# Layer 0's denominators and normalised tokens turned by VectorE instead of TensorE, its projection placed at the next block's end, and layer 1's query rows copied by ScalarE

## The chip, the cores and the metric

The kernel runs on one core of a Trainium2 chip. The metric is the device time of the whole program in microseconds: 2126.64 us is the median of three runs of the kernel before (2126.23 to 2128.68). The span of its profile is 2126.2 us. A core has TensorE (PE, matmuls; its weight loads are listed apart as PEld), VectorE (DVE), ScalarE (ACT), GpSimd (POOL), and a sync engine (SP) that issues most transfers. The engines work through their own instructions in order and wait for one another through semaphores.

## The reference, cut to what matters

The input x is 4 images of 128 channels and 64 x 64 = 4096 tokens, all float32. Two layers of attention follow each other, and then a recurrent layer.

```python
# layer 0: attention over all tokens, 64 channels, residual in channel layout
att = jax.nn.softmax(jnp.einsum('bmi,bmj->bij', k, q), axis=2)
out = x + jnp.einsum('cm,bmn->bcn', wo, jnp.einsum('bij,bmj->bmi', att, v))
...
# layer 1: causal attention over normalised tokens, 128 channels
t = t + _L1_attn_ref(_ln_t(t), L1_attn_Wq, L1_attn_Wk, L1_attn_Wv)
# then a normalisation, a batch norm of W x and a scan over the tokens
t = t + _L1_ffn_ref(_ln_t(t), L1_ffn_W, L1_ffn_V, L1_ffn_gamma, L1_ffn_beta)
```

`_ln_t` subtracts the mean and divides by the standard deviation over the 128 channels of one token. What the change touches is the end of layer 0's attention: each token's weighted sum of values is projected by `wo`, divided by its softmax denominator and added to the token, and the result is normalised for layer 1.

## The kernel before, in words

`fast_path` (from L350) is what runs here. For each of the four batches it goes through layer 0 and then layer 1 in blocks of 512 queries, eight blocks per layer (g = 0 to 7). A block consists of items; an item is a pair of key tiles of 128 keys each, so p, the exponentials of one item, is 128 x 1024 for full tiles. Layer 0 has 16 items in each block. Layer 1 is causal and has 2, 4, ... 16 items in blocks 0 to 7; its last two items cross the diagonal and are narrower.

Every item passes through four steps:

- `scores` (L741 in layer 0, L750 in layer 1): TensorE multiplies keys by queries into a PSUM pair, of which there are two. Layer 0 has 64 channels only, so it uses 64 x 64 tiles of the array, four at a time.
- the exp by ScalarE (L755, L757) into p, which has four buffers (`prob`, bufs=4). In layer 1 GpSimd masks the diagonal (L761).
- `sums` (L779 the first item of a block, L781 the others): VectorE adds p up into `dsum`, from which the softmax denominators come.
- `values` (L801, L809): TensorE multiplies values by p and accumulates in `acc`, which has one buffer.

At the end of a layer-0 block ScalarE copies `acc` to `half` (L820), VectorE adds its two halves into `agg` (L821) and the two halves of `dsum` into `den` (L825). `den` is 128 x 512: it still has to be summed over the 128 partitions for each of 512 queries, and the result has to stand with a query on each partition.

The order of the work is that of the loop at the end of `fast_path`'s attention part. One turn of it is a slot. In slot s it emits the scores of item s, the values of item s - 2, then, where that item was the last of its block, `rows()` (the queries of the block after the next), `tokens()` (the load of tokens), and one task from the list `fill`; then it pushes the block's finishing chain (`finish0` or `finish1`). After that come the sums of item s and at most one due step of a finishing chain, or else one task of `side` (keys and values of the next batch). A chain is a generator; the number that it yields with a step says how many slots later the step is due. The framework then settles the place of each instruction on its engine; it may bring an instruction ahead of others on the same engine.

Before the change, `finish0` has one step, due two slots after the block's end: `project`, then `norm`. In layer 0 `project` has TensorE transpose `den` in four 128 x 128 pieces (L572), VectorE sums them from PSUM (L573) and takes reciprocals (L574); TensorE multiplies `agg` by `wo` (L577) and VectorE scales and adds to the tokens in `xs` (L582). `normed` takes mean and variance (L591, L592), has GpSimd raise the variance to the power -0.5 (L455), refines this by a Newton step on VectorE (L456 to L459), and writes normalised tokens `xh` (L598). At the next block's end the task from `fill` has TensorE transpose `xh` (L606), and ScalarE copies it to `xhT` (L607). In layer 1 `xhT` serves as keys and, multiplied by `g1` in `rows1` (L548, copied by VectorE, L550), as queries.

In layer 1 `project` already goes another way: VectorE transposes `den` in squares of 32 x 32 (L561), sums each (L563, `part`, 128 x 16), TensorE adds up the four partition groups with the constant matrix `fold` (L564), and VectorE picks the own group (L566, L569). Layer 1's normalised tokens go through squares as well: `second` in `finish1` transposes squares (L674, `sqT`), and DMAs write them to DRAM as `by_c` and read them back (L679, L683) so that the squares come to their places.

All of `r_ps`, `den_ps`, `o_ps`, `xhT_ps`, `wx_ps` and the tiles of keys and values come from one PSUM pool with two buffers (`misc`).

Of the kernel before, what the change touches and what calls it, by code (L numbers as in the profile page):

```python
# [9 lines left out]
F32 = mybir.dt.float32  # L10
AF = mybir.ActivationFunctionType
ALU = mybir.AluOpType
AX = mybir.AxisListType
PSUM = bass.MemoryType.PSUM

P = 128
BLK = 512
# [332 lines left out]
def fast_path(  # L350
# [21 lines left out]
    nc = tc.nc  # L372
# [5 lines left out]
    TPB = BLK // P  # L378
# [5 lines left out]
    S = nc.vector.STREAM_SQUARE_SIZE  # L384
    Q = P // S
# [4 lines left out]
    dram2 = ctx.enter_context(tc.tile_pool(name="dram2", bufs=2, space=bass.MemoryType.DRAM))  # L390
# [24 lines left out]
    ident = const.tile([P, P], F32, name="ident")  # L415
# [10 lines left out]
    fold = const.tile([P, P], F32, name="fold")  # L426
# [6 lines left out]
    quarter = const.tile([P, TPB, Q], F32, name="quarter")  # L433
# [27 lines left out]
    with tc.tile_pool(name="batch", bufs=1) as batch, tc.tile_pool(name="rows", bufs=2) as rowp, tc.tile_pool(  # L461
        name="prob", bufs=4
    ) as prob, tc.tile_pool(name="work", bufs=2) as wk, tc.tile_pool(name="stat", bufs=4) as stat, tc.tile_pool(
        name="ps_s", bufs=2, space=PSUM
# [81 lines left out]
        def rows1(b, g):  # L546
            ps = misc("r_ps")
            nc.tensor.matmul(ps, lhsT=g1, rhs=bs[b].xhT[:, ts(g, BLK)], start=True, stop=True)  # L548
            r = rowp.tile([P, BLK], F32, tag="r", name="rows1")
            nc.vector.tensor_copy(r, ps)  # L550
            bs[b].next.append(r)

        def project(layer, b, g, agg, den):

            dp = misc("den_ps")
            rec = recs[:, layer, b, ts(g, TPB)]
            if layer:


                sq = wk.tile([P, TPB * Q, S], F32, tag="sq", name="sq")  # L560
                nc.vector.transpose(out=sq.rearrange("p a b -> p (a b)"), in_=den)  # L561
                part = stat.tile([P, TPB * Q], F32, tag="part", name="part")
                nc.vector.tensor_reduce(part, sq, AX.X, ALU.add)  # L563
                nc.tensor.matmul(dp[:, : TPB * Q], lhsT=fold, rhs=part, start=True, stop=True)  # L564
                own = stat.tile([P, TPB, Q], F32, tag="own", name="own")
                nc.vector.tensor_tensor(  # L566
                    own, dp[:, : TPB * Q].rearrange("p (j q) -> p j q", q=Q), quarter, ALU.mult
                )
                nc.vector.tensor_reduce(rec, own, AX.X, ALU.add)  # L569
            else:  # L570
                for j in range(TPB):
                    nc.tensor.transpose(dp[:, ts(j, P)], den[:, ts(j, P)], ident)  # L572
                nc.vector.tensor_reduce(rec, dp.rearrange("p (j k) -> p j k", k=P), AX.X, ALU.add)  # L573
            nc.vector.reciprocal(rec, rec)  # L574
            op = misc("o_ps")
            for j in range(TPB):
                nc.tensor.matmul(  # L577
                    op[:, ts(j, P)], lhsT=agg[:, ts(j, P)], rhs=wv1 if layer else wo2, start=True, stop=True
                )
            for j in range(TPB):  # L580
                t = xs[:, b, ds(g * BLK + j * P, P)]
                nc.vector.scalar_tensor_tensor(  # L582
                    t, in0=op[:, ts(j, P)], scalar=rec[:, j : j + 1], in1=t, op0=ALU.mult, op1=ALU.add
                )
# [17 lines left out]
        def transposed(src, dst, name, engine):  # L602

            ps = misc(name)
            for j in range(TPB):
                nc.tensor.transpose(ps[:, ts(j, P)], src[:, j], ident)  # L606
            engine(dst, ps)  # L607

        def in_range():

            r = recs.rearrange("p l b t -> p (l b t)")
            r2 = wk.tile([P, BLK], F32, tag="den", name="r2")[:, : 2 * B * NT]
            nc.vector.tensor_scalar(r2, r, LOW, None, ALU.is_ge)
            nc.vector.tensor_scalar(r, r, HIGH, None, ALU.is_le)
            nc.vector.tensor_tensor(r, r, r2, ALU.mult)
            nc.vector.tensor_reduce(good, r, AX.X, ALU.add)
# [8 lines left out]
        def finish0(b, g):  # L625

            agg, den = bs[b].agg, bs[b].den

            def norm():
                if g == 0:  # L630
                    bs[b].xh = batch.tile([P, NT, P], F32, tag="xh", name="xh")
                    bs[b].xhT = batch.tile([P, N], F32, tag="xhT", name="xhT")
                normed(b, g, bs[b].xh[:, ts(g, TPB)])

            yield 2, lambda: (project(0, b, g, agg, den), norm())
            fill.append(
                lambda: transposed(bs[b].xh[:, ts(g, TPB)], bs[b].xhT[:, ts(g, BLK)], "xhT_ps", nc.scalar.copy)
            )

        def finish1(b, g):  # L640
            agg, den = bs[b].agg, bs[b].den
            mem = {}
            final = b == B - 1 and g == NB - 1

            def warm(n, rhs):

                ps = ps_s.tile([P, 2 * BLK], F32, tag="s", name="warm_ps")
                for _ in range(n):
                    nc.tensor.matmul(ps[:, : BLK // 2].rearrange("p (a c) -> p a c", c=P) if len(rhs.shape) == 3 else ps[:, : BLK // 2], lhsT=ident, rhs=rhs, start=True, stop=True)

            def first():
                if final:

                    nc.scalar.activation(spare, agg[:, 0:1], AF.Sigmoid)
                project(1, b, g, agg, den)
                if final:
                    warm(9, agg[:, : BLK // 2])
                nc.sync.dma_start(
                    out=x2[b, ts(g, BLK)].rearrange("(j p) c -> p j c", p=P),
                    in_=xs[:, b, ts(g, BLK)].rearrange("p (j c) -> p j c", c=P),  # L660
                )
                mem["xh"] = wk.tile([P, TPB, P], F32, tag="xh2", name="xh2")
                normed(b, g, mem["xh"])

            def second():
                mem["xhT"] = wk.tile([P, BLK], F32, tag="xhT2", name="xhT2")
                if final:
                    transposed(mem["xh"], mem["xhT"], "xh2T_ps", nc.vector.tensor_copy)
                    warm(1, mem["xh"][:, 2:])
                    return  # L670


                sq = wk.tile([P, Q, TPB, S], F32, tag="sqT", name="sqT")
                nc.vector.transpose(  # L674
                    out=sq.rearrange("p c j t -> p j c t"), in_=mem["xh"].rearrange("p j (c r) -> p j c r", r=S)
                )
                by_c = dram2.tile([Q, S, Q, P], F32, tag="by_c", name="by_c")
                for q in range(Q):
                    nc.sync.dma_start(  # L679
                        out=by_c[:, :, q].rearrange("c r k -> r c k"),  # L680
                        in_=sq[ts(q, S)].rearrange("r c j t -> r c (j t)"),
                    )
                nc.sync.dma_start(out=mem["xhT"], in_=by_c.rearrange("c r q k -> (c r) (q k)"))  # L683

            def third():
                wp = misc("wx_ps")
                nc.tensor.matmul(wp, lhsT=wf, rhs=mem["xhT"], start=True, stop=True)
                if b == B - 1 and g == NB - 1:
                    in_range()
                nc.vector.bn_stats(ends[:, 3:] if final else stats[:, b * NB + g], wp)  # L690
                if b == B - 1 and g == NB - 2:
                    ahead()

                to = xs[:, b, ts(g, BLK)]
                if final:
                    nc.scalar.copy(to.rearrange("p (s c) -> p s c", c=CPB), wp.rearrange("p (c s) -> p s c", s=STEPS))
                    warm(6, to[:, : BLK // 2])
                else:
                    nc.scalar.copy(  # L699
                        to.rearrange("p (s j q u) -> p s j q u", q=Q, j=TPB, s=STEPS),  # L700
                        wp.rearrange("p (q j u s) -> p s j q u", q=Q, j=TPB, s=STEPS),
                    )

            yield 1, first
            yield 3, second
            yield 1 if final else 4, third
# [123 lines left out]
        def push(slot, chain):  # L830
            step = next(chain, None)
            if step:
                waiting.append((slot + step[0], step[1], chain))
# [39 lines left out]
        for s in range(len(items) + SKEW + 16):  # L873
# [8 lines left out]
            if 0 <= s - SKEW < len(items):  # L882
                it = items[s - SKEW]
                values(it)
                if it.last:
                    rows()
                    tokens()
                    if fill:
                        fill.pop(0)()
                    push(s, (finish1 if it.layer else finish0)(it.b, it.g))  # L890
            if s < len(items):
                sums(items[s])
# [174 lines left out]
```

## Time and profile before

| what | from | value |
|---|---|---|
| span of the profiled execution | page | 2126.2 us |
| ScalarE, exps of layer 0, 512 of 128 x 1024 | L755 | 1117 ns each |
| VectorE, sums, 676 of 128 x 1024 | L781 | 1224 ns each |
| VectorE, denominators from PSUM, layer 0 | L573 | 684 ns x 32 |
| VectorE, squares of den, layer 1 | L561 | 711 ns x 32 |
| VectorE, sums of the squares, layer 1 | L563 | 677 ns x 32 |
| VectorE, own group, and its sum, layer 1 | L566, L569 | 169 and 168 ns x 32 |
| VectorE, squares of tokens, layer 1 | L674 | 711 ns x 31 |
| copy of r: VectorE | L550 | 680 ns x 32 |
| copy of the transposed tokens: ScalarE, same shape | L607 | 596 ns x 32 |
| TensorE, transposes of den and of tokens | L572, L606 | 128 each |

In a row of a timeline the first number is the start in us from the start of the span, the second the duration, then come engine, line, operation, what is written from what, the shape, and how many instructions are merged into the row. What stands in brackets is the idle time of the engine before it and who ended it. A float32 matmul counts as two records. Records of consecutive matmuls overlap in time, so that the distance of two starts says what the first cost, not its duration. In a row of stretches each engine has the us in which it was busy and the number of instructions.

### The profile page before, as it was taken

The numbers are of one execution on the slowest core, as the hardware profiler recorded it, in microseconds if no ns is written. First come the engines' busy times: TensorE is split into PE (matmuls) and PEld (weight loads), VectorE is DVE, ScalarE is ACT, GpSimd is POOL, SyncE is SP. The second block draws the span as 40 slices with busy tenths as digits, with TensorE's granted clock in tenths as the row PEclk, the third lists the DMA queues.
The fourth block names the chain that finished last, engine by engine and source line by source line (L and its number), as shares of the span: only waits on it lengthen the run. The fifth ranks groups of instructions, "written<-read, shape, count | busy, mean of one in ns | idle before, by whom it ended". The sixth has DMA issues, their size and how long they took to land. (4 is left out here: it accounts for less than half of the span.)

```text
span 2126.2 us, 30582 instructions
## 1 busy us (share of the span) xinstructions
PE 2102.6 (99%) x12072; PEld 931.3 (44%) x12072; DVE 1467.1 (69%) x2810; ACT 1009.4 (47%) x1099; POOL 110.2 (5%) x220
## 2 busy tenths in 40 slices
PE   9999999999999999999999999999999999999998
PEld 3333354444333344444333335444433334544456
DVE  4888865555888876544688887555478887755478
ACT  5666633233666643323466663332356664332355
POOL 1000000000000000000000001000000000100000
PEclk9999999999999999999999999999999999999999
DMA  3100022000100002100010002200000000110043
GB/s 110 41 1 2 1 60 60 15 15 16 55 2 1 2 21 69 35 25 15 16 41 1 2 1 60 60 15 15 15 16 1 1 2 1 45 30 15 15 164 160
DMA packets 66167, 64.98 MB, mean 31 GB/s; under 512 B 5617, under 2 KB 54257, under 8 KB 64993
## 3 DMA queue, kind: packets, MB, share of 16 engines
q1 hardware_dynamic: 65008, 62.41, 9.4%
q8 instruction: 96, 1.57, 0.3%
q14 instruction: 55, 0.44, 0.1%
q0 software_dynamic: 288, 0.39, 0.1%
q10 hardware_dynamic: 720, 0.16, 0.0%
HBM read 33.85 MB, written 24.90 MB: 28 GB/s over the span
## 5 line engine op out<-in xcount | busy, mean ns | idle before, releaser
L781 DVE TENSOR_TENSOR dsum<-dsum,p 128x1024 f32<-128x1024 f32 x676 | 827.3, 1224 | 454.1 <-ACT p L757 319.0
L755 ACT ACTIVATE p<-s_ps,nshift 128x1024 f32<-128x1024 f32 x512 | 572.0, 1117 | 349.4 <-PE s_ps L741 330.4
L757 ACT ACTIVATE p<-s_ps 128x1024 f32<-128x1024 f32 (+2 forms) x288 | 274.7, 954 | 563.7 <-PE s_ps L750 538.5
L801 PE MATMUL acc<-p,v 64*64 64x512 f32 x4096 | 533.9, 591 | 1.7 <-ACT half L820 1.7
L741 PE MATMUL s_ps<-kr 64*64 64x512 f32 x2048 | 530.4, 595 | 0.0
L741 PE MATMUL s_ps<-swap,kr 64*64 64x512 f32 x2048 | 530.4, 595 | 0.0
L750 PE MATMUL s_ps<-rows,xhT 128*128 128x512 f32 (+3 forms) x1152 | 503.1, 559 | 1.4 <-DVE rows L550 1.4
L809 PE MATMUL acc<-p,xh 128*128 128x512 f32 (+3 forms) x1152 | 501.5, 557 | 0.0
L809 PEld LDWEIGHTS acc<-p,xh 128*128 128x128 f32 x1152 | 215.6, 190 | 241.3 <-issue 231.8
L750 PEld LDWEIGHTS s_ps<-rows,xhT 128*128 128x128 f32 x1152 | 212.9, 190 | 242.3 <-issue 196.2
L801 PEld LDWEIGHTS acc<-p,v 64*64 64x64 f32 x4096 | 155.3, 133 | 286.1 <-issue 267.1
L741 PEld LDWEIGHTS s_ps<-swap,kr 64*64 64x64 f32 x2048 | 136.8, 133 | 132.4 <-issue 124.0
L741 PEld LDWEIGHTS s_ps<-kr 64*64 64x64 f32 x2048 | 136.9, 133 | 128.3 <-issue 123.7
L455 POOL TENSOR_TENSOR ln_rstd<-ln_var,mhalf 128x4 f32<-128x4 f32 x64 | 65.8, 1028 | 1086.5 <-DVE ln_var L594 1075.6
L789 DVE TENSOR_TENSOR dsum<-dsum,p 128x256 f32<-128x256 f32 (+1 forms) x120 | 55.9, 500 | 74.3 <-POOL p L761 74.3
L582 DVE SCALAR_TENSOR_TENSOR xs<-o_ps,recs,xs 128x128 f32<-128x128 f32 x256 | 72.5, 345 | 9.1 <-PE o_ps L577 3.1
L598 DVE TENSOR_SCALAR xh<-xs,ln_mv,ln_rstd 128x128 f32<-128x128 f32 x256 | 71.4, 344 | 2.2
L761 POOL TENSOR_SCALAR_AFFINE_SELECT p<-p 128x128 f32<-128x128 f32 x128 | 34.6, 294 | 665.5 <-ACT p L757 651.9
L591 DVE BATCH_NORM_STATS2 ln_st<-xs 128x6 f32<-128x128 f32 x256 | 63.7, 273 | 0.0
L779 DVE COPY dsum<-p 128x1024 f32<-128x1024 f32 x60 | 41.4, 690 | 29.8 <-ACT p L757 26.6
L699 ACT COPY xs<-wx_ps 128x512 f32<-128x512 f32 x31 | 18.2, 587 | 83.3 <-DVE stats L690 76.4
L964 DVE SCALAR_TENSOR_TENSOR z<-xs,scale,y_ps 128x256 f32<-128x256 f32 x108 | 48.3, 481 | 3.4 <-PE y_ps L962 1.9
(138 smaller groups left out, 1068.7 us busy)
## 6 DMA issues: line engine op xcount, KB each, us to landing
xs<-in_xT SPq DMA_DIRECT2D x32, 256.0 KB, 3.0
x<-xs SPq DMA_DIRECT2D x32, 256.0 KB, 2.2
xr<-x SPq DMA_DIRECT2D x8, 1024.0 KB, 12.1
out_x<-xr SPq DMA_DIRECT2D x16, 512.0 KB, 3.4
by_c<-sqT SPq DMA_DIRECT2D x124, 64.0 KB, 1.7
xhT<-by_c SPq DMA_DIRECT2D x31, 256.0 KB, 2.7
xs<-in_x SPq DMA_DIRECT2D x12, 512.0 KB, 5.5
swap<-kr SPq DMA_DIRECT2D x32, 128.0 KB, 2.2
```

What stands on the lines that cost most here:

```text
L455: nc.gpsimd.tensor_tensor(y, var, mhalf[:, : y.shape[-1]], ALU.pow)
L582: nc.vector.scalar_tensor_tensor(t, in0=op[:, ts(j, P)], scalar=rec[:, j : j + 1], in1=t, op0=ALU.mult, op1=ALU.add)
L591: nc.vector.bn_stats(st[:, j], xs[:, b, ds(g * BLK + j * P, P)])
L598: nc.vector.tensor_scalar(dst[:, j], xs[:, b, ds(g * BLK + j * P, P)], mv[:, j, 0:1], y[:, j : j + 1], ALU.subtract, ALU.mult)
L741: nc.tensor.matmul(ps[c * M : c * M + M, off : off + n], lhsT=bs[it.b].kr[part, h, ds(t % (NT // 2) * P + c * M, M)], rhs=rows[h], start=True,
L750: nc.tensor.matmul(ps[:, off : off + n], lhsT=lhsT, rhs=rhs, start=True, stop=True)
L755: nc.scalar.activation(it.p[:, :off], ps[:, :off], AF.Exp, bias=nshift)
L757: nc.scalar.activation(it.p[:, :off], ps[:, :off], AF.Exp, scale=float(P) ** -0.5)
L781: nc.vector.tensor_tensor(flat, flat, it.p, ALU.add)
L789: nc.vector.tensor_tensor(den[:, h, q0:], den[:, h, q0:], it.p[:, o : o + n], ALU.add)
L801: nc.tensor.matmul(bt.acc[h * M : h * M + M, r], lhsT=bt.v[part, t], rhs=it.p[part, o : o + n], start=it.first, stop=it.last,)
L809: nc.tensor.matmul(bt.acc[:, 0, q0:], lhsT=bt.xh[:, t], rhs=it.p[:, o : o + n], start=it.first and h == 0, stop=it.last and h == 1,)
```

## The change

The first four parts concern what follows a layer-0 block, the last one layer 1:

- `folded` holds the squares of `den` and their sums, which stood in layer 1's `project`; layer 0 now uses it too. `project` takes its result `part` in both layers, and the four transposes of `den` on TensorE and the reduce from PSUM go.
- `finish0`'s first step, one slot after the block's end, is `folded` alone; the projection is put into `fill` and so comes at the next block's end, between the last values of that block and the next scores.
- The norm follows one slot after the projection, and the transposition of the tokens two slots after that.
- Tokens are transposed in squares by VectorE (`squares`, which layer 1's `second` now calls too), and four DMAs write them to `by_r` in DRAM in pieces of 32 values (128 B), four more read `xhT` from there. The four transposes on TensorE and the copy by ScalarE go.
- `rows1` has ScalarE copy r, not VectorE.

Its purpose is to take transposes off TensorE, which the profile shows busy 99% of the span.

```diff
             r = rowp.tile([P, BLK], F32, tag="r", name="rows1")
-            nc.vector.tensor_copy(r, ps)
+            nc.scalar.copy(r, ps)
...
-        def project(layer, b, g, agg, den):
+        def folded(den):
+            sq = wk.tile([P, TPB * Q, S], F32, tag="sq", name="sq")
+            nc.vector.transpose(out=sq.rearrange("p a b -> p (a b)"), in_=den)
+            part = stat.tile([P, TPB * Q], F32, tag="part", name="part")
+            nc.vector.tensor_reduce(part, sq, AX.X, ALU.add)
+            return part
+        def project(layer, b, g, agg, part):
...
-            if layer:
...
-            else:
-                for j in range(TPB):
-                    nc.tensor.transpose(dp[:, ts(j, P)], den[:, ts(j, P)], ident)
-                nc.vector.tensor_reduce(rec, dp.rearrange("p (j k) -> p j k", k=P), AX.X, ALU.add)
+            nc.tensor.matmul(dp[:, : TPB * Q], lhsT=fold, rhs=part, start=True, stop=True)
...
-            yield 2, lambda: (project(0, b, g, agg, den), norm())
-            fill.append(
-                lambda: transposed(bs[b].xh[:, ts(g, TPB)], bs[b].xhT[:, ts(g, BLK)], "xhT_ps", nc.scalar.copy)
-            )
+            def by_channels():
+                sq = squares(bs[b].xh[:, ts(g, TPB)])
+                by_r = dram2.tile([S, Q, TPB, Q, S], F32, tag="by_r", name="by_r")
+                for q in range(Q):
+                    nc.sync.dma_start(
+                        out=by_r[:, :, :, q].rearrange("r c j t -> r (c j) t"),
+                        in_=sq[ts(q, S)].rearrange("r c j t -> r (c j) t"),
+                    )
+                for c in range(Q):
+                    nc.sync.dma_start(
+                        out=bs[b].xhT[ts(c, S), ts(g, BLK)], in_=by_r[:, c].rearrange("r j q t -> r (j q t)")
+                    )
+            def rest():
+                yield 1, norm
+                yield 2, by_channels
+            def first():
+                part = folded(den)
+                def second(s):
+                    project(0, b, g, agg, part)
+                    push(s, rest())
+                fill.append(second)
+            yield 1, first
...
-                        fill.pop(0)()
+                        fill.pop(0)(s)
```

More of the change, by code (lines that the diff above doesn't have):

```diff
@@ L549, in rows1 @@
             r = rowp.tile([P, BLK], F32, tag="r", name="rows1")
-            nc.vector.tensor_copy(r, ps)
+            nc.scalar.copy(r, ps)
             bs[b].next.append(r)
-        def project(layer, b, g, agg, den):
+        def folded(den):
[5 more added lines that the diff above has]
+        def project(layer, b, g, agg, part):
             dp = misc("den_ps")
             rec = recs[:, layer, b, ts(g, TPB)]
-            if layer:
[L560 to L567, printed above, removed]
-                )
-                nc.vector.tensor_reduce(rec, own, AX.X, ALU.add)
-            else:
-                for j in range(TPB):
-                    nc.tensor.transpose(dp[:, ts(j, P)], den[:, ts(j, P)], ident)
-                nc.vector.tensor_reduce(rec, dp.rearrange("p (j k) -> p j k", k=P), AX.X, ALU.add)
+            nc.tensor.matmul(dp[:, : TPB * Q], lhsT=fold, rhs=part, start=True, stop=True)
+            own = stat.tile([P, TPB, Q], F32, tag="own", name="own")
+            nc.vector.tensor_tensor(own, dp[:, : TPB * Q].rearrange("p (j q) -> p j q", q=Q), quarter, ALU.mult)
+            nc.vector.tensor_reduce(rec, own, AX.X, ALU.add)
             nc.vector.reciprocal(rec, rec)
@@ L607, in transposed, with squares @@
             engine(dst, ps)
+        def squares(src):
+            sq = wk.tile([P, Q, TPB, S], F32, tag="sqT", name="sqT")
+            nc.vector.transpose(out=sq.rearrange("p c j t -> p j c t"), in_=src.rearrange("p j (c r) -> p j c r", r=S))
+            return sq
         def in_range():
@@ L633, in norm @@
                 normed(b, g, bs[b].xh[:, ts(g, TPB)])
-            yield 2, lambda: (project(0, b, g, agg, den), norm())
-            fill.append(
-                lambda: transposed(bs[b].xh[:, ts(g, TPB)], bs[b].xhT[:, ts(g, BLK)], "xhT_ps", nc.scalar.copy)
-            )
+            def by_channels():
[20 more added lines that the diff above has]
+            yield 1, first
         def finish1(b, g):
@@ L654, in first @@
                     nc.scalar.activation(spare, agg[:, 0:1], AF.Sigmoid)
-                project(1, b, g, agg, den)
+                project(1, b, g, agg, folded(den))
                 if final:
@@ L670, in second @@
                     return
[L673 to L676, printed above, removed]
+                sq = squares(mem["xh"])
                 by_c = dram2.tile([Q, S, Q, P], F32, tag="by_c", name="by_c")
```

## The prediction

> **What bounds the kernel now.** I read the page's first two parts, then the table by stretches, then the timelines of single blocks. First part 1 of the page, then two stretches (a layer-0 block, and the first blocks of layer 1):
>
> ```profile
> PE 2102.6 (99%) x12072; PEld 931.3 (44%) x12072; DVE 1467.1 (69%) x2810; ACT 1009.4 (47%) x1099; POOL 110.2 (5%) x220
> ```
>
> ```profile
> 82.00:112.00 30.00, 30.00 (x280) 11.44 (x276) 25.13 (x42) 19.23 (x18) 1.01 (x1) 1.00 0.01 1
> 262.00:290.00 28.00, 27.66 (x108) 14.60 (x105) 19.63 (x65) 9.95 (x14) 4.16 (x10) 1.00 0.14 38
> ```
>
> Columns of the stretches: TensorE, weight loads, VectorE, ScalarE, GpSimd busy. TensorE never rests, so removed TensorE work should shorten the run; but in layer 0 VectorE is already at 25.1 of 30 us. How much each part of a block costs TensorE is read from starts in its timeline (block 2 of batch 0):
>
> ```profile
> 81.91 1.04 PE L801 MATMUL acc<-p,v 64*64 64x512 f32 x8
> 82.88 0.66 PE L606 MATMUL xhT_ps<-ident,xh 128*128 128x128 f32 x4
> 83.47 0.65 PE L741 MATMUL s_ps<-swap,kr 64*64 64x512 f32 x2
> ...
> 84.38 1.04 PE L801 MATMUL acc<-p,v 64*64 64x512 f32 x8
> ...
> 86.10 1.04 PE L801 MATMUL acc<-p,v 64*64 64x512 f32 x8
> 87.06 0.66 PE L572 MATMUL den_ps<-ident,den 128*128 128x128 f32 x4
> 87.56 1.06 PE L577 MATMUL o_ps<-wo,agg 128*128 128x128 f32 x8
> 88.54 0.65 PE L741 MATMUL s_ps<-swap,kr 64*64 64x512 f32 x2
> ...
> 89.45 1.04 PE L801 MATMUL acc<-p,v 64*64 64x512 f32 x8
> ```
>
> From L801 to L801 an undisturbed item takes 1.72 (84.38 to 86.10). The block end with the token transposes takes 2.47, so 0.75 extra; the one with denominators and projection 3.35, so 1.63 extra. A block is 16 x 1.717 + 0.75 + 1.63 = 29.85; the den instructions (L825) at 81.14 and 110.99 are 29.85 apart. VectorE in that block:
>
> ```profile
> 83.31 1.22 DVE L781 TENSOR_TENSOR dsum<-dsum,p 128x1024 f32<-128x1024 f32 x1 [0.88 <-ACT p L755]
> ...
> 85.78 1.23 DVE L781 TENSOR_TENSOR dsum<-dsum,p 128x1024 f32<-128x1024 f32 x1 [0.64 <-ACT p L755]
> ...
> 87.49 1.23 DVE L781 TENSOR_TENSOR dsum<-dsum,p 128x1024 f32<-128x1024 f32 x1 [0.49 <-ACT p L755]
> ...
> 93.21 0.16 DVE L456 TENSOR_TENSOR ln_z<-ln_rstd 128x4 f32<-128x4 f32 x1 [1.13 <-POOL ln_rstd L455]
> ...
> 96.05 13.19 DVE L781 TENSOR_TENSOR dsum<-dsum,p 128x1024 f32<-128x1024 f32 x10
> 109.73 1.23 DVE L781 TENSOR_TENSOR dsum<-dsum,p 128x1024 f32<-128x1024 f32 x1 [0.49 <-ACT p L755]
> ```
>
> The ten sums from 96.05 run without a wait: VectorE is behind after the norm and works off its arrears at 1.33 per sum against 1.72 per item. It waits for ScalarE's p only four times, 0.88 + 0.64 + 0.49 + 0.49 = 2.5, of which some 0.05 each is ordinary issue. So 2.3 us in a block is all the slack VectorE has; the 1.13 for GpSimd's power stays in any case.
>
> **The skill.** "Perfetto Trace Analysis", Identifying the Most-Contended Engine, says that matmul busy share is a poor measure because matmuls are pipelined. The trace agrees (records of 1.04 every 0.86), so I count starts, not busy time. "VectorE: DVE Perf Modes", The three transpose paths, says that VectorE transposes 32x32 blocks only and TensorE a full 128x128; here that is why the new tokens path needs a trip through DRAM to put blocks in place. "DMA: Bandwidth & Descriptors", the specifications table and Why small descriptors are slow, names 512 B as the size for line rate and a fixed cost per packet; this trace has no 128 B store of this kind, only by_c with 512 B pieces, 64 KB in 1.7 us.
>
> **The change, part by part, on TensorE.** Removed in layer 0: four denominator transposes (87.06 to 87.56, 0.50) and four token transposes (with their change of tile shape and what remains of the wait for half, 0.75). Added: the fold matmul, which in layer 1 starts 0.14 before the o matmuls (278.81 to 278.95). The o matmuls stay at 0.98 but move to the next block's end, where the token transposes stood, so the change of tile shape (0.10 before, 0.05 after) is paid once: 0.10 + 0.14 + 0.98 + 0.05 = 1.27. This place also hides ScalarE's half copy. At the end of block 0, where nothing stands there before or after the change, the L801 starts are 52.15 and 54.47, an extra of 0.60 for half. With 1.27 in between, half (1.27 after the last L801's start, 1.01 long) ends at 2.28 while the next L801 would start at 0.86 + 1.27 + 0.86 = 2.99. TensorE's need of a block falls from 29.85 to 16 x 1.717 + 1.27 = 28.74. The part is ready a block earlier, so the fold adds no wait there.
>
> **VectorE.** The block's need before is 29.85 - 2.3 = 27.55. Removed: the 512-wide reduce, 0.72 (88.63 to 89.35). Added, by layer 1's rows: transpose of den 0.71, its reduce 0.68, own 0.17, its reduce 0.17, transpose of the tokens 0.71: 2.44. In the built order the transposes follow what they read, one more sum stands in the chain of dependent sums (1.33 instead of 1.14), and no sum fills the gaps between the small rstd steps; by the starts of the same pairs in layer 1 I put this at 0.4. 27.55 - 0.72 + 2.44 + 0.4 = 29.65. That is above TensorE's 28.74: VectorE becomes the bound in layer 0. Bounds: 29.3 (no such waits) to 30.0 (double).
>
> How it reaches TensorE: p has four buffers, so the exp of item n+4 waits for the sum of item n. Counted from the start of the last L801 of a block, the built order on VectorE is the last sum (at -2.0), den, its transpose and reduce, first copy, a sum, own, agg, o-add, statistics, a sum, power, tokens, transpose: 13.7 us, so the fourth item's sum (item 3) starts at 11.7 and ends at 12.9. The exp that needs its buffer is due at 11.9 and goes about 1 us late; scores two items on use its PSUM pair and still fit. So a block without arrears does not stall; it leaves VectorE 29.65 - 28.74 = 0.9 behind, and from then on each block stalls by 0.9 and lasts 29.65.
>
> **Rows and DMA.** The copy of r moves from VectorE (0.68) to ScalarE (0.59), 32 of each. ScalarE is half idle; behind the copy stands the next exp, whose scores come later than r. Where a block end has r, fold and o, two shared PSUM buffers serve three tiles: o waits for the copy, which stands behind half. Ends: r at 0.96 to 1.82, half until 2.28, copy until 2.9, o due at 2.1, so about 0.6 to 0.8 of wait, with the next item's scores and so the next exps queued behind it; this is at block 6's end (in block 7's period) of each batch. The eight DMAs of a block run while the DMA share is 0.01; xhT of block g is first read by TensorE at the end of the sixth block after it, about 100 us or more after its stores start, and sqT is overwritten two blocks later. I cost them at nothing, hidden by those blocks' matmuls; even at four times by_c's 1.7 us for each store (an estimate: four times the pieces) a block needs under 40 us.
>
> **Sum per batch**, before against after, by periods between block ends. Block 1: 29.76 (den starts 51.38 to 81.14), after 16 x 1.717 + 0.60 = 28.07: -1.69. Block 2, no arrears yet: -1.11. Blocks 3 to 6 at VectorE's 29.65: 4 x -0.2 = -0.8. Block 7 also has r: before 30.76 (230.42 to 261.18), after TensorE 28.74 + 0.86 + 0.6 = 30.2: -0.56. Entry to layer 1: one block's 0.5 denominator and 0.43 token transposes go, fold and waits of about 0.6 come: -0.3. Together -4.5, four batches -18: 2126.6 - 18 = 2109.
>
> **Rivals.**
> TensorE stays the bound (20%): VectorE's waits shrink when it has arrears, and it keeps up. Block periods 2 to 6 at 28.74: -1.69 - 5 x 1.11 - 0.56 - 0.3 = -8.1, four batches -32: 2094. For it: TensorE's 99%. Against: the 2.3 us of slack, against 1.1 lost to the shorter block and 2.1 of added work.
> VectorE needs more, no change (9%): at 30.5 per block, as when each new dependent pair waits longer, blocks 2 to 6 cost 4 x 0.65 - 1.11 = +1.5 instead of -1.9; -1 per batch: 2122, and a little more brings 2126. Against: every added row exists in layer 1 with a stable duration.
> Slower (8%): in layer 1 r, fold, o, wx and the keys share two PSUM buffers, and ScalarE's copy now stands behind exps and agg. If each of seven block ends stalls 1 us more for it, or wx waits for a transpose held up behind the small stores, +7 - 4.5 = +2.5 per batch: 2137. For it: wx already waits for its DMA three times, 5.6 us in the waits. Against: half the copies land where ScalarE idles, and VectorE's own copies made TensorE wait too (L750 for rows, 4 times).
> The main case has 63%: 2109, with 29.3 and 30.0 giving about 2103 and 2115.
>
> The range must take in TensorE's case and the upper bound: 2091 to 2122 leaves out the last two, 17%. Faster 0.84, same 0.09, slower 0.07.
>
> **What would show it.** Right: in layer 0 the den starts lie 29.6 to 29.7 apart from block 3 on and 28.1 to 28.8 in blocks 1 and 2; VectorE busy above 26.5 of 30 us with hardly a wait for p but with exps waiting for dsum; no transposes on TensorE in layer 0. Wrong on the bound: spacing of 28.7 throughout with VectorE waiting for p. Wrong on rows: PE waits for ScalarE's rows in layer 1, or for DMA at wx, longer than before.

## The result, and the profile after

The changed kernel takes 2116.89 us (median of four runs, 2116.39 to 2118.44), the kernel before beside it 2126.73 (2126.23 to 2128.68). The ratio is 0.9953, with a 95% interval of 0.9938 to 0.9968: the change gains about 10 us where 18 were forecast. In the profiles the spans are 2126.2 and 2115.1 us, 11.1 apart.

Part 1 of the page of the kernel after, busy time and instructions of each engine:

```profile
PE 2081.9 (98%) x11880; PEld 918.3 (43%) x11880; DVE 1501.6 (71%) x2906; ACT 1009.5 (48%) x1099; POOL 112.2 (5%) x220
```

TensorE has 192 matmul records fewer: 256 for the transposes are gone, 64 for layer 0's fold have come. VectorE has 34.5 us more. Where that matters is seen in a single stretch, block 4 of layer 0 in the first batch (columns as before: TensorE, weight loads, VectorE, ScalarE, GpSimd busy; then the granted TensorE clock, the DMA engines' busy share and GB/s):

```profile
138.00:168.00 30.00, 29.70 (x278) 11.04 (x274) 27.11 (x47) 18.83 (x18) 1.01 (x1) 1.00 0.09 19
```

In layer 0 VectorE went from 25.13 (before, this stretch has the same as the one shown there) to 27.11 of 30 us, and TensorE, which had never rested there, now rests 0.3 us. VectorE's timeline of the block from 109.02 to 138.50 shows that it has no time left:

```profile
109.02 0.69 DVE L848 TENSOR_TENSOR den<-dsum 128x512 f32<-128x512 f32 x1
109.75 0.71 DVE L556 STREAM_TRANSPOSE sq<-den 128x512 f32<-128x512 f32 x1
110.49 0.69 DVE L558 TENSOR_REDUCE part<-sq 128x16 f32<-128x512 f32 x1
...
118.75 0.16 DVE L456 TENSOR_TENSOR ln_z<-ln_rstd 128x4 f32<-128x4 f32 x1 [1.13 <-POOL ln_rstd L455]
...
120.69 0.71 DVE L609 STREAM_TRANSPOSE sqT<-xh 128x512 f32<-128x512 f32 x1
121.33 17.13 DVE L804 TENSOR_TENSOR dsum<-dsum,p 128x1024 f32<-128x1024 f32 x13
138.50 0.69 DVE L848 TENSOR_TENSOR den<-dsum 128x512 f32<-128x512 f32 x1
```

The only wait in brackets is the one for GpSimd's power. The four waits for p that gave VectorE 2.3 us of slack before are gone; thirteen sums run one after another, up to the next den, 29.48 after the last. The waits of the kernel after (us in total, times, longest) show the other side:

```profile
ACT p L778 <- DVE dsum L804: 50.9, 58, 2.6
...
DVE dsum L804 <- ACT p L778: 70.0, 107, 2.0
...
PEld o_ps L574 <- DVE own L569: 10.8, 8, 2.0
...
PE wx_ps L710 <- DMA xhT<-by_c: 5.6, 3, 1.9
```

Exps wait for the sums that free their buffer, 50.9 us in all. No such line stands among the waits of layer 0 before, where no exp waited more than 0.6 us for VectorE. VectorE's own waits for p in layer 0 fell from 105.5 to 70.0 us. The third line is new and is taken up below. The fourth, layer 1's wait for a transfer, is that of before, so no disturbance by the eight transfers per block shows there.

TensorE at the end of block 1, to set beside the two block ends of before:

```profile
80.21 1.04 PE L824 MATMUL acc<-p,v 64*64 64x512 f32 x8
81.18 0.40 PE L567 MATMUL den_ps<-part,fold 128*128 128x16 f32 x2
81.42 1.14 PE L574 MATMUL o_ps<-wo,agg 128*128 128x128 f32 x8
82.49 0.65 PE L764 MATMUL s_ps<-swap,kr 64*64 64x512 f32 x2
...
83.40 1.04 PE L824 MATMUL acc<-p,v 64*64 64x512 f32 x8
```

From L824 to L824 it is 3.19, so 1.47 more than an undisturbed item of 1.717. TensorE's need of a block is 16 x 1.717 + 1.47 = 28.94.

**Where the time went.** A block's length is read from the starts of ScalarE's copies to `half` (L820 before, L843 after), one at each block end. Layer 0 of the third batch, in us:

| kernel | 1 | 2 | 3 | 4 | 5 | 6 | 7 |
|---|---|---|---|---|---|---|---|
| before | 29.76 | 29.85 | 29.86 | 29.86 | 29.86 | 29.86 | 31.76 |
| after | 28.12 | 28.94 | 29.15 | 29.48 | 29.47 | 29.47 | 33.05 |

Block 7 also has r and the first scores of layer 1 (before, it is 31.76 by these copies and 30.76 by den's starts, which the prediction used). In the other batches one or two of blocks 4 to 6 take 29.82 instead of 29.47. The mean over the four batches, in us per batch, beside the terms of the prediction:

| term | predicted | measured |
|---|---|---|
| block 1 | -1.69 | -1.64 |
| block 2 | -1.11 | -0.92 |
| blocks 3 to 6 | -0.8 | -1.49 |
| block 7 | -0.56 | +1.29 |
| layer 1 with its entry | -0.3 | -0.09 |
| sum | -4.5 | -2.9 |

Four batches of -2.86 are -11.4; the start, the batches' joints and the end of the program add 0.3, which gives the 11.1 of the spans. One term has the wrong sign, block 7. What holds it up stands in the timeline of the kernel after around the end of block 6:

```profile
227.19 1.04 PE L824 MATMUL acc<-p,v 64*64 64x512 f32 x8
227.27 0.69 DVE L848 TENSOR_TENSOR den<-dsum 128x512 f32<-128x512 f32 x1
...
228.15 1.12 PE L548 MATMUL r_ps<-xhT,g 128*128 128x512 f32 x2
...
229.12 0.29 PE L567 MATMUL den_ps<-part,fold 128*128 128x16 f32 x2
229.34 0.60 ACT L550 COPY rows<-r_ps 128x512 f32<-128x512 f32 x1
...
230.13 1.23 DVE L804 TENSOR_TENSOR dsum<-dsum,p 128x1024 f32<-128x1024 f32 x1
231.27 0.16 DVE L569 TENSOR_TENSOR own<-den_ps,quarter 128x16 f32<-128x16 f32 x1
...
231.49 1.16 PE L574 MATMUL o_ps<-wo,agg 128*128 128x128 f32 x8 [1.08 <-DVE own L569]
```

The o matmuls were due at 229.4, 0.24 after the fold. ScalarE's copy of r is done at 229.94, and still they start at 231.49, just after VectorE's `own` (231.27 to 231.43), which reads the fold's result. `own` has nothing to wait for by then but stands in VectorE's queue behind den, its transpose, its reduce, the first copy and a sum. Behind o stand the next scores, all but a first pair of matmuls, and behind those the exps.

### The profile page after: what moved, and what is told of

Same layout as the page of the kernel before. It is cut to its first block, busy times and chain, and to the rows that moved or that the text cites. A ratio compares the mean times of both kernels' runs of the same rounds, so it can differ in the third digit from the quotient of the medians.

```text
span 2115.1 us, 30710 instructions
## 1 busy us (share of the span) xinstructions
PE 2081.9 (98%) x11880; PEld 918.3 (43%) x11880; DVE 1501.6 (71%) x2906; ACT 1009.5 (48%) x1099; POOL 112.2 (5%) x220
## 5 line engine op out<-in xcount | busy, mean ns | idle before, releaser
L764 PE MATMUL s_ps<-kr 64*64 64x512 f32 x2048 | 570.4, 594 | 5.0 <-ACT p L778 5.0
L824 PE MATMUL acc<-p,v 64*64 64x512 f32 x4096 | 572.9, 592 | 1.7 <-ACT half L843 1.7
L824 PEld LDWEIGHTS acc<-p,v 64*64 64x64 f32 x4096 | 169.4, 133 | 281.9 <-issue 274.0
L764 PEld LDWEIGHTS s_ps<-kr 64*64 64x64 f32 x2048 | 152.3, 133 | 143.6 <-issue 122.4
```

Source lines behind the costliest of these rows:

```text
L764: nc.tensor.matmul(ps[c * M : c * M + M, off : off + n], lhsT=bs[it.b].kr[part, h, ds(t % (NT // 2) * P + c * M, M)], rhs=rows[h], start=True,
L824: nc.tensor.matmul(bt.acc[h * M : h * M + M, r], lhsT=bt.v[part, t], rhs=it.p[part, o : o + n], start=it.first, stop=it.last,)
```

## The experiments

My theory after the result: VectorE's need sets blocks 3 to 6, and block 7 is lost to o's wait for `own`. The rivals: TensorE or p's path through PSUM still sets the blocks; block 7 is lost to r's place or its copy. Each ratio is to the kernel before, run on the same chip. All block lengths are of the third batch; where another batch differs by more than 0.4, the text says so.

### A sum less and a sum more

In layer 0, in the kernel after (one edit each):

```diff
+            if it.layer == 0 and it.k == 8:      # one sum less
+                return
...
                     nc.vector.tensor_tensor(flat, flat, it.p, ALU.add)
+                    if it.layer == 0 and it.k == 8:      # one sum more
+                        nc.vector.tensor_tensor(flat, flat, it.p, ALU.add)
```

One sum less:

> The changed kernel, leaving out VectorE's sum of the ninth item in every layer-0 block (the denominators lack that item). Theory (VectorE sets blocks 3 to 6): its need falls by 1.33 from 29.47 to 28.14, below TensorE's 28.94, so the periods of blocks 2 to 6 all become 28.94 and the wait for own at block 7 shrinks by some 0.9; per batch about -2.0 - 0.9, time 2106. Rival (TensorE or the order at block ends sets the period, VectorE only looks full): periods stay at 29.5, time 2116 to 2117.

One sum more:

> The changed kernel, adding the ninth item's p twice in every layer-0 block (the denominators count that item double): VectorE gets 1.33 us more per block. Theory: each steady block grows by all of it, to 30.8; about five blocks per batch, block 7 too, so +7 per batch and 2145. Rival (VectorE has slack left): blocks grow by less than 0.4, time under 2125.

The same sum more in the kernel before:

> The kernel before with the ninth item's p added twice into the denominators in each layer-0 block (the output is wrong by that): 1.33 us more for VectorE in a block. The same edit cost the changed kernel 1.26 us in each steady block, 31.5 us in all. Theory (VectorE had 2.3 us of slack in a block of 29.85, TensorE sets the time): layer-0 blocks stay at 29.86, time within 2 of 2126.7. Rival (VectorE was the bound, or its arrears reach p's buffers, before the change too): up to 1.3 per block, 2140 to 2160.

| kernel | us | ratio (95%) | 1 | 2 | 3 | 4 | 5 | 6 | 7 |
|---|---|---|---|---|---|---|---|---|---|
| after, a sum less | 2102.17 | 0.9884 (0.9867 to 0.9900) | 28.12 | 28.94 | 28.94 | 28.94 | 28.94 | 28.94 | 32.19 |
| after, a sum more | 2148.38 | 1.0104 (1.0087 to 1.0121) | 28.12 | 28.94 | 30.41 | 30.73 | 30.72 | 31.08 | 35.87 |
| before, a sum more | 2128.95 | 1.0008 (1.0001 to 1.0015) | 29.76 | 29.86 | 29.86 | 29.86 | 29.86 | 29.86 | 31.76 |

With a sum less blocks 2 to 6 are all at TensorE's 28.94; with a sum more a steady block grows by 1.26. In the kernel before the same 1.33 us of added work changed no block by more than 0.01, and the time by 0.08%. So VectorE's slack before was real, and with four buffers for p it is VectorE's need that sets blocks 3 to 6 after.

Block 7 is 0.86 shorter with a sum less and 2.82 longer with a sum more. With a sum less VectorE is not late at all: den starts 2.04 before the copy to `half` at the ends of blocks 0 to 6, as in the kernel before. Yet o still waits for `own` at the end of block 6:

```profile
228.82 0.17 DVE L569 TENSOR_TENSOR own<-den_ps,quarter 128x16 f32<-128x16 f32 x1
...
229.04 1.16 PE L574 MATMUL o_ps<-wo,agg 128*128 128x128 f32 x8 [0.23 <-DVE own L569]
```

The fold starts at 227.53 there, so o was due at 227.77 and comes 1.27 late. In the kernel after it comes 2.13 late. So 1.27 of that is due to `own`'s place in VectorE's order, behind the work on the new den, and 0.86 to VectorE being late.

The times were 4 us better and 3 us worse than expected. With a sum less, most of that lies between the batches, where the trace of the kernel after twice has 3.4 us at half the TensorE clock and this run has none: those two joints are 3.5 us shorter together. With a sum more it is block 7, which the section on r's copy comes back to.

### The projection a slot later where it meets r

```diff
+                    with_r = it.layer == 0 and blocks and blocks[0][0] == 1
                     rows()
                     tokens()
-                    if fill:
+                    if fill and with_r:
+                        waiting.append((s + 1, lambda task=fill.pop(0), n=s + 1: task(n), iter(())))
+                    elif fill:
                         fill.pop(0)(s)
```

> The changed kernel, with one edit: at the two block ends of a batch where layer 1's r and layer 0's projection meet (layer 0's blocks 6 and 7), the projection comes one slot later, r stays. Theory: in block 7's period the o matmuls stand about 2.1 us because they take the PSUM buffer of the fold's result, which VectorE's own reads only after its arrears (copy, a sum). A slot later r's buffer is free, so block 7's period (half to half) falls from 33.05 to about 31.8 and the time by 4 x 1.2 = 5 us, to about 2112. Rival: block 7 is long because VectorE is behind on p as in blocks 3 to 6; then the period stays at 32.7 to 33.1 and the time within 1 us of 2117.

2110.85 us, 0.9920 (0.9904 to 0.9937), 1 us from what was expected. Block 7 falls from 33.05 to 31.16, blocks 1 to 6 are within 0.02 of those of after. TensorE's timeline of this kernel at the end of block 6 and one item later:

```profile
227.38 1.04 PE L824 MATMUL acc<-p,v 64*64 64x512 f32 x8
228.35 1.12 PE L548 MATMUL r_ps<-xhT,g 128*128 128x512 f32 x2
...
230.31 1.04 PE L824 MATMUL acc<-p,v 64*64 64x512 f32 x8
231.28 0.40 PE L567 MATMUL den_ps<-part,fold 128*128 128x16 f32 x2
231.53 1.14 PE L574 MATMUL o_ps<-wo,agg 128*128 128x128 f32 x8
```

o follows the fold after 0.25, without a wait, and among the waits none of o for `own` is left (10.8 and 4.3 us after). r, alone now, costs 2.93 - 1.717 = 1.21. The 1.89 us per batch, 7.6 in four, are more than the gain measured between the two kernels (6, or 7 by the ratios): layer 1 with its entry takes 0.8 us more in each of the first three batches.

### Who copies r

In the kernel after, r copied by VectorE as before; and in the kernel before, r copied by ScalarE as after (the reverse of this edit):

```diff
-            nc.scalar.copy(r, ps)
+            nc.vector.tensor_copy(r, ps)
```

> The changed kernel with r copied by VectorE again, as before the change. Theory (o waits for VectorE's own, not for r's copy): block 7's period does not shorten; VectorE gets 0.68 us more in it, so it stays at 33.0 or grows by up to 0.7; time 2116 to 2120. Rival (the wait comes from ScalarE's copy of r, which stands behind half): period falls by 1 to 2 us, time 2109 to 2113.

> The kernel before with one part of the change: r copied by ScalarE. Theory: before the change no projection stands behind r at a block end (only token transposes), VectorE has 2.3 us of slack, so the copy's engine costs or brings little: time 2124 to 2128. Rival (r's copy by VectorE held TensorE up before, too): four to eight us less, 2119 to 2123.

The first takes 2122.80 us, 0.9978 (0.9971 to 0.9984), more than expected; the second 2125.19, 0.9994 (0.9985 to 1.0003), not to be told from the kernel before, with layer 0's blocks unchanged to 0.01 and the entry to layer 1 0.6 shorter. Block 7 of the first takes 35.19, and as much in two other batches, but 33.57 in the second. Its waits:

```profile
PEld o_ps L574 <- DVE rows L550: 17.7, 12, 2.5
PE o_ps L574 <- DVE rows L550: 8.6, 9, 1.6
```

Now it is the copy of r that o waits for, since that copy stands in VectorE's queue. In each batch o comes 0.5 later than in the kernel after, and in the second batch block 7 is longer by just that. In the other three the granted TensorE clock is at half for 3.4 us after the wait. The 10 us around it in the first and in the second batch (the third number from the end is the clock):

```profile
230.00:240.00 10.00, 8.39 (x58) 3.26 (x60) 7.14 (x24) 2.73 (x3) 1.01 (x1) 0.83 0.00 0
736.50:746.50 10.00, 8.39 (x74) 3.72 (x76) 8.03 (x28) 3.73 (x4) 1.01 (x1) 1.00 0.00 0
```

Half the clock for 3.4 us costs TensorE 1.7 us, and 1.62 is what block 7 takes beyond 33.57. The same is seen with a sum more, in all four batches: TensorE rests 2.3 us before o, o comes 1.27 later than in the kernel after, and block 7 is 2.82 longer. In the kernel after, with a rest of 1.1 us, the clock stays whole. Why the second batch here escaped with the same rest of 1.6 us was not looked into.

So the move of this copy is worth nothing by itself and some 5 to 6 us together with the rest of the change, most of it through the clock: o waits for whatever of the two stands in VectorE's queue. Which of the two shared buffers o is given can only be told from who released it; after the change that was `own`, here it is `rows`.

### A fifth buffer for p

`prob`, bufs=5 instead of 4: alone, and with the later projection.

```diff
-name="prob", bufs=4
+name="prob", bufs=5
```

> The changed kernel with five p buffers instead of four. Theory (VectorE lacks throughput, the buffers only say when TensorE feels it): blocks 2 and 3 at 28.94, later ones at 29.47 again, block 7's wait for own longer by what the arrears grew; time within 2 us of 2117. Rival (a burst of VectorE work, which one more buffer would carry): all blocks at 28.94 and 2107 to 2109.

> The kernel with the projection one slot later where it meets r, with five buffers for p instead of four. With five buffers alone VectorE's arrears grew until block 7, where the projection waited for own and paid all of it (block 7 took 36.4 us). Theory: that payment came from o's wait for own; with the projection a slot later there is less of it, so blocks 2 to 6 stay at 28.94 to 29.0 and block 7 takes 32 to 33: about 0.2 + 1.5 - 1.3 = 0.4 us less per batch than without the fifth buffer: 2109. If no wait for own is left (31.2 in block 7), the arrears are carried into layer 1, where VectorE has time, and the gain is 1.7 per batch: 2104. Rival (arrears are always paid in full by the end of the batch's layer 0): 2111.

| kernel | us | ratio (95%) | 1 | 2 | 3 | 4 | 5 | 6 | 7 |
|---|---|---|---|---|---|---|---|---|---|
| fifth buffer | 2119.40 | 0.9969 (0.9956 to 0.9981) | 28.12 | 28.94 | 28.94 | 28.94 | 28.94 | 29.01 | 36.39 |
| fifth buffer, later projection | 2102.39 | 0.9883 (0.9867 to 0.9900) | 28.12 | 28.94 | 28.94 | 28.94 | 28.94 | 29.02 | 31.16 |

The pair separates the two waits. With the fifth buffer VectorE may be one item further behind before an exp has to wait, and blocks 3 to 5 come out at TensorE's need although VectorE's is higher (block 6 too in the third batch; it takes 29.36 to 29.71 in the others). The debt is not gone: at block 6's end den starts 0.54 after the copy to `half`, in the kernel after 1.18 before it, which is one item later. There o waits for a later `own`, 3.7 us at the longest instead of 2.0. It comes 1.71 later than in the kernel after, which is what blocks 3 to 6 gained (1.74), and half the clock for 3.4 us follows in all four batches: block 7 takes 36.39, 3.34 more. What the buffer brought is paid there and the clock comes on top; the time is 2.5 us longer than that of the change, within the intervals. With the projection a slot later nothing at that place asks for VectorE's work; block 7 takes 31.16 as without the fifth buffer. VectorE needs some 29.5 per block, so in block 7, which is longer than that, it begins to catch up, and layer 1 takes no longer than with four buffers. Of the three cases that were expected it is the best one, and 2 us better. It is the fastest kernel of the study that leaves no sum out, 1.2% faster than the kernel before. Exps still wait for sums, but less than half as long (23.7 us in 33 waits, for the 50.9 in 58 of after). In the first batch block 6 takes 29.49.

### Taking work off VectorE

The sum of `half`'s two halves on GpSimd, with the later projection:

```diff
-                    nc.vector.tensor_tensor(bt.agg, half[:, 0], half[:, 1], ALU.add)
+                    nc.gpsimd.tensor_tensor(bt.agg, half[:, 0], half[:, 1], ALU.add)
```

> The kernel with the projection one slot later where it meets r, and besides the sum of half's two halves into agg (L844, 0.69 us of VectorE in each layer-0 block) on GpSimd. Nobody waits for agg until the next block's end. Theory (in blocks 3 to 6 VectorE's own need, 29.47 us, sets the time): VectorE's need falls to about 28.8, below TensorE's 28.94, so the half copies lie 28.94 apart in blocks 2 to 6 and about 31.0 in block 7: 0.2 + 3 x 0.5 + 0.2 = 1.9 us per batch, 2110.9 - 8 = 2103. Rival (something else holds blocks 3 to 6, as p's buffers through TensorE and ScalarE): no change, 2111. Rival (an addition on GpSimd disturbs VectorE's own while it runs): 2111 to 2115.

2113.18 us, 0.9932 (0.9915 to 0.9948): no gain over the later projection alone (0.9920, and the intervals overlap). The main expectation, 2103, missed; the rival on disturbance holds. Timelines of this kernel, VectorE's and then GpSimd's, at the same block end:

```profile
141.20 2.11 DVE L804 TENSOR_TENSOR dsum<-dsum,p 128x1024 f32<-128x1024 f32 x1
143.23 0.16 DVE L569 TENSOR_TENSOR own<-den_ps,quarter 128x16 f32<-128x16 f32 x1
```

```profile
140.88 1.34 POOL L844 TENSOR_TENSOR agg<-half 128x512 f32<-128x512 f32 x1 [23.69 <-ACT half L843]
```

While GpSimd adds, VectorE's sum takes 2.11 instead of 1.22; the two meet in this way in the steady blocks of the first batch, from the end of block 3 on. What left VectorE, 0.41 between the reciprocal and the tokens' update (0.27 instead of 0.68), is less than the 0.89 that this sum grew. VectorE's period, from den to den, is 29.91 (138.34 to 168.25) instead of 29.47. In the other batches VectorE's addition begins first at the ends of blocks 1 to 3; there it takes 1.23 and GpSimd's 2.1 to 2.3, and VectorE's period is 29.04. That is still above TensorE's 28.94, so VectorE gets a little later with each block, until GpSimd's addition begins first and VectorE's takes 2.1 to 2.3. Block lengths agree: 28.94 in blocks 2 to 4 but 29.56 and 29.92 in blocks 5 and 6 (in the first batch 29.62 already in block 4).

The last step of layer 0's norm on ScalarE, alone and with the later projection:

```diff
+            if act:
...
+                nc.vector.scalar_tensor_tensor(nb, in0=mv[:, :, 0], scalar=-1.0, in1=y, op0=ALU.mult, op1=ALU.mult)
+                for j in range(TPB):
+                    nc.scalar.activation(
+                        dst[:, j], xs[:, b, ds(g * BLK + j * P, P)], AF.Identity, scale=y[:, j : j + 1], bias=nb[:, j : j + 1]
+                    )
+                return
...
-                normed(b, g, bs[b].xh[:, ts(g, TPB)])
+                normed(b, g, bs[b].xh[:, ts(g, TPB)], act=True)
```

> The changed kernel, with layer 0's last step of the norm (four 128x128 of VectorE, 1.03 us from start to start) done by ScalarE as an Identity with scale and bias; VectorE makes the bias in one small instruction of 0.2. Theory (VectorE's need of 29.47 sets the blocks): need about 28.6, below TensorE's 28.94, so blocks 3 to 6 fall to 28.94 and block 7 to about 32.2 as when a sum was left out; time 2103. Rival (ScalarE, with half and four more instructions between exps, delays p): blocks stay above 29.3, time 2113 or more.

> Both repairs: the projection one slot later where it meets r, and layer 0's last norm step on ScalarE. If the two causes are separate, the gains add: blocks 3 to 6 at 28.94, block 7 at 31.0 to 31.2; per batch -2.0 and -1.9 against the changed kernel, time about 2101. If they are one cause (VectorE's arrears), the second repair adds nothing to the first in block 7 and the time stays at 2103 to 2105.

2267.19 us, 1.0667 (1.0649 to 1.0684), and 2268.81, 1.0672 (1.0654 to 1.0690): both 7% slower and far from what was expected. ScalarE's timeline in block 2 of the first of them:

```profile
83.72 1.12 ACT L786 ACTIVATE p<-s_ps,nshift 128x1024 f32<-128x1024 f32 x1 [1.17 <-PE s_ps L772]
90.33 1.65 ACT L598 ACTIVATE xh<-xs,ln_nb,ln_rstd 128x128 f32<-128x128 f32 x4 [5.50 <-DVE ln_nb L596]
91.89 2.09 ACT L786 ACTIVATE p<-s_ps,nshift 128x1024 f32<-128x1024 f32 x2
```

The four small instructions stand ahead of two exps and wait 5.5 us for VectorE's `ln_nb`. Exps, scores and values stop behind them, and blocks 2 to 6 take 35.5 to 37.1. Part of this is TensorE's clock, which is at half for 3.4 or 6.8 us after such waits: its mean is 0.973 in this run and 0.997 in the kernel after. By that, some 54 of the 150 us lost are the clock's (an estimate: 0.024 of 2263 us). I had counted the instructions and not the wait in front of them. So these two tell nothing of VectorE's need; whether the step would pay if it were emitted some slots later was not tried.

### The denominators without the tokens

The kernel after with the tokens' transposes on TensorE and the copy on ScalarE, at the place where the squares would be:

```diff
             def by_channels():
-                sq = squares(bs[b].xh[:, ts(g, TPB)])
...
+                transposed(bs[b].xh[:, ts(g, TPB)], bs[b].xhT[:, ts(g, BLK)], "xhT_ps", nc.scalar.copy)
```

> The changed kernel with layer 0's tokens transposed by TensorE and copied by ScalarE as before (placed where the squares would be), so that only the denominators, the later projection and the copy of r are changed. Theory (VectorE sets the changed kernel's blocks 3 to 6): VectorE's need falls by 0.71 to 28.8, TensorE's rises from 28.94 by 0.5 to 0.75 to some 29.5 to 29.7, so blocks 2 to 6 take 29.5 to 29.7 and block 7 about 32, since own is less late: 2117, within 3 of the whole change. Taking the token transposes off TensorE then brought nothing. Rival (TensorE's work is what counts): 28 blocks x 0.65 us more, 2135.

2225.38 us, 1.0461 (1.0444 to 1.0479); both expectations missed. TensorE in block 2, from the timeline of that kernel:

```profile
87.27 1.04 PE L814 MATMUL acc<-p,v 64*64 64x512 f32 x8
...
90.90 1.25 PE L603 MATMUL xhT_ps<-ident,xh 128*128 128x128 f32 x4 [2.59 <-DVE xh L595]
...
93.84 1.19 PE L814 MATMUL acc<-p,v 64*64 64x512 f32 x8
```

From L814 to L814 it is 6.57, 4.85 over an undisturbed item, and blocks 2 to 7 take about 34.3 (33.95 to 35.72 over all batches). Of the 4.85 the wait is 2.59, and 1.7 is the clock, which is at half for 3.4 us from 90.7 on. The norm comes only two slots earlier, its result is not there, and TensorE waits in order with everything behind it. So the run doesn't separate the tokens' part from the denominators', as it was meant to; that split stays open. It does show what the squares and transfers bring besides: nobody on TensorE waits for a block's tokens when the norm is late.

## Why the prediction was right and where it was not

**Right: the bound.** VectorE became the bound of blocks 3 to 6, and blocks 1 and 2 came at TensorE's pace, as the steps said: 28.12 (said: 28.07) and 28.94. The runs with a sum less and a sum more show it. By the sign that the prediction named, the distance of den's starts, only block 1 is free: it is 29.47 already in block 2 (29.59 in the first batch), where VectorE falls behind without TensorE feeling it yet. VectorE's need was put at 29.65 (the terms add up to 29.67) and is 29.47. If the other terms hold, 0.2 of the 0.4 added for longer chains of dependent work was there; this was not measured apart.

**Off in size: TensorE's need.** 28.74 was said, 28.94 measured. The block end costs 1.47 rather than 1.27: the fold's start lies 0.24 before o's, not 0.14 as in layer 1, and the o matmuls take 1.07 up to the next scores, not 0.98.

**Off in size: blocks 3 to 6.** -0.8 was said, -1.5 measured. With 29.47 and 28.94 a block leaves VectorE 0.53 behind instead of 0.9, and block 3 still runs at 29.15: p's four buffers held more of the arrears than I had allowed. This error and that of block 7 have opposite signs and in part cancel in the sum.

**Wrong: block 7.** The step "about 0.6 to 0.8 of wait", for ScalarE's copy of r at the end of block 6, named the wrong releaser. It followed o's buffer back to r and its reader on ScalarE, and did not ask about the fold's reader. That reader is on VectorE, and the prediction's own list of VectorE's order has it behind den, its transpose, its reduce, a copy and a sum. The wait is 2.13 us in place of 0.6 to 0.8. As the run with a sum less shows, 1.27 of it would have come with a VectorE in time, and 0.86 came from its arrears. Block 7 came to +1.29 instead of -0.56; 1.85 x 4 = 7.4 us, of the 8 by which the time missed. Moving o by one slot took 1.89 out of block 7 and the wait out of the list, which settles this.

**Right: transfers and rows.** The small stores were costed at nothing; the wait of wx is 5.6 us before and after. Of the slower rival's stalls in layer 1, o's wait for r's copy is there, but at 1.7 us in all; layer 1 is as long as before to 0.1 us per batch. What the entry gains (1.28 in three batches) later blocks of layer 1 give back (1.14 in all, single ones between -2.6 and +5.1); why was not looked into.

**The rivals.** TensorE's case (2094) did not come, but the fastest kernel shows it at 2102: blocks 2 to 6 at 28.94 to 29.02 (one of 29.49 in the first batch), once a fifth buffer carries VectorE's debt and nothing collects it before block 7 is through.

## What to carry to other kernels

When a change puts a reader on a busy engine, go through every wait for that engine, however small the instruction, and look at its place in the order as well as at the engine's lateness: a 0.16 us `own` behind a full queue cost four times 1.9 us because the matmuls behind it needed its buffer. A deeper buffer only postpones the debt of a late engine; it pays where a stretch with slack follows and nothing in between asks for that engine's result. Before moving work to an idle engine, look for what its first instruction waits for and what is queued behind it: waits of 5.5 and 2.6 us made two moves cost 5 to 7%, about a third of it through the slower TensorE clock after them.

## What the runs showed of the hardware that was not expected

- An addition of 128 x 512 float32 on GpSimd takes 1.82 us in the mean of 32 (VectorE: 0.69), and one of VectorE's 128 x 1024 additions beside it took 2.11 instead of 1.22. Whichever of the two begins first is hardly slowed (at the ends of blocks 1 to 6 VectorE 1.23, GpSimd 1.27 to 1.63), and the other then takes 2.1 to 2.3.
- Stores of 64 KB to DRAM in pieces of 128 B land 2.2 us after their issue (median of 128), those in pieces of 512 B after 1.8: pieces of a quarter of the size, but not four times the time.
- The first 128 x 128 matmul after 64 x 64 tiles starts 0.97 after the last values' start instead of 0.86, and the fold with its 16 columns still holds TensorE for 0.24.
- The granted TensorE clock fell to half for 3.4 us after rests of 2.3 us or more at the end of block 6 (with a sum more, with a fifth buffer) in all four batches, after a rest of 1.6 us in three of four, and after the rest of 1.1 us in the kernel after in none. It made block 7 some 1.6 us longer each time.
